# A routed LoRA, attention and nearest-neighbour chain on one core: distances in the two row halves of the array, keys early, dummy products first

## The chip, the core and the metric

The kernel runs on one core of a Trainium2 chip. The core has a matrix engine (TensorE, PE in the profile; its weight loads are shown apart as PEld), a vector engine (VectorE, DVE), a scalar engine (ScalarE, ACT), a general engine (GpSimd, POOL) and a queue that issues transfers (SyncE, SP). Each runs its own instructions in order and they meet at semaphores. The metric is the device time of one execution in microseconds (us), as the median of several.

## What is computed

There are 4 batches of 256 rows of 512 features (`x`), 64 context vectors of 512 features for each batch (`ctx`), four 256 x 256 matrices (`fside`) and a mask over the context vectors. In outline:

```
A   = ctx[0] + ctx[1] + ctx[2] + ctx[3]                             # 64 x 512
x   = x + 0.5 * sum_n softmax(x Rw^T + b)_n * ((x A^T) B_n^T)        # 8 experts, rank 64; then nan and inf are replaced
q, k, v = x Wq^T + bq,  ctx Wk^T + bk,  ctx Wv^T + bv               # 32 heads of 16
x   = layernorm(x + softmax(q k^T / 4, masked) v Wo^T + bo)
idx = for each of the 512 columns of ctx (64 numbers each): the 8 nearest columns
8 times, with matrix i mod 4:
    p = leaky_relu(x)                                              # x as 256 channels by 512 points
    x = x + (F_i p + F_i * (sum of p over the 8 neighbours)) / 9
```

The "points" of the last part are the 512 feature columns. Their positions are the columns of `ctx` of the same batch, 64 x 512. The neighbours are the same in all 8 rounds, so a 512 x 512 matrix of zeros, ones and (because each point is its own nearest neighbour and also enters on its own) twos on the diagonal, `nbr`, is made once for each batch, and each round is two matrix products.

## The kernel before

**The stages.** `mixture` and `mix` are the routed LoRA: `route` (x times router and summed A), on VectorE a softmax over experts and z (the softmax weights times the rank-64 part), z transposed (`zT`), `upd` with `lora_BT`, and x updated; hi, lo, odd and copy_predicated (L436 to L440) replace nan and inf, hi + lo on POOL. `x1T` is x transposed for the queries. `keys` makes `kT` and from it the block-wise keys `kbd` for all batches at once; `values`, `queries` and `attention` follow for each batch: scores `s` as row-quarter products (four products of 32 rows side by side in the array, each with `tile_position`), softmax on VectorE and ScalarE with the last multiplication on POOL (L716), transposes `pT`, `avT`, `o` with Wo, layer norm (its last two operations on POOL, L784 and L785). `block` is one of the 8 rounds of a batch: p on VectorE (L798), `wp` = p times F (fp32, L809), its two parts as float32r: `wph` rounded on ScalarE (L822) and the rest `wpl` on VectorE (L825), `blk` = both parts times `nbr` (L840), x updated (L852).

**The distances.** `nearest` (L459) makes `nbr`. The eight nearest columns m of a column n are those with the largest x_n . x_m - |x_m|^2 / 2. For this the moving operand `cxx` holds the 64 rows of ctx and below them their squares (ScalarE, L460), and the weights `cxl` hold the 64 rows again (a copy on POOL, L461) and below them -0.5 (set by POOL, L280). One fp32 product with 128 rows per 128 columns n, two passes in the profile, gives the tile `d` (L469). VectorE takes the eight largest of each row (`top`) and replaces them by a very low number (`rest`), ScalarE makes ones of these (`near`, bf16), TensorE transposes them and adds the diagonal (`nbrT`, L499 and L501), and ScalarE stores `nbr`. A batch has four tiles `d`.

**The order.** No order is written by hand. `Plan` (L57) records every operation with its engine, a cost, what it reads and what it writes. `emit` then goes through them as a list scheduler: for each engine it finds the operations that could start first (by the end of what they depend on, plus `SEEN[engine]`, a latency that is counted where a result is used on another engine), takes among these the one with the lowest rank, and of the engines' choices the earliest. The rank is `DEADLINES[batch]` less the longest remaining chain of work in that batch (for all operations of a round, of that round), so a batch with a low due time goes first. PSUM has 8 banks; an operation that needs one waits until one is free, and a second count, "stage", says how many may be held by tiles of everything but the block stage. Loads are all issued on SP in the order in which they are written (L253 to L274), and each waits for the one eight before it.

**The start.** The first load is 64 rows of ctx of batch 0. `d` of batch 0 needs it squared and copied. `route` of batch 0 needs its xT and the summed A. Each of the four pieces of Wk (`WkT`, 256 KB) holds 128 input features for all outputs, so that the first `kT` needs all four.

Of the kernel before, what the change touches and what calls it, by code (L numbers as in the profile page):

```python
# [8 lines left out]
F32 = mybir.dt.float32  # L9
BF16 = mybir.dt.bfloat16  # L10
F32R = mybir.dt.float32r
U8 = mybir.dt.uint8
I32 = mybir.dt.int32
AF = mybir.ActivationFunctionType
ALU = mybir.AluOpType
AX = mybir.AxisListType

B, S, H = 4, 256, 512
V, R = 64, 64
# [3 lines left out]
NC = H // 128  # L23
# [5 lines left out]
SLOPE = 0.01  # L29
LN_EPS = 1e-5  # L30
LOW = -3.0e38
DEADLINES = (0.0, 5.0, 10.0, 15.0)

SEEN = {"PE": 0.2, "ACT": 0.15, "DVE": 0.1, "POOL": 0.12, "SP": 0.0}


LANES = 8
RATE = 0.3  # L40

# [15 lines left out]
class Plan:  # L57
# [33 lines left out]
    def emit(self, deadline):  # L91
        longest = {}
        for op in reversed(self.ops):
            op.tail = op.cost + max(
                [o.tail + (SEEN[op.eng] if o.eng != op.eng else 0.0) for o in op.after if o.batch == op.batch],
                default=0.0,
# [6 lines left out]
        for op in self.ops:  # L103
            if op.rank is None:
                op.rank = deadline[op.batch] - longest.get(op.unit, op.tail)
        free = dict.fromkeys(SEEN, 0.0)
        ready = [op for op in self.ops if not op.todo]
# [47 lines left out]
def xattn_seq_kernel(ctx: ExitStack, tc: tile.TileContext, a: dict, out: bass.AP):  # L155
    nc = tc.nc
    V_, G_, A_, T_, S_ = nc.vector, nc.gpsimd, nc.scalar, nc.tensor, nc.sync

    const = ctx.enter_context(tc.tile_pool(name="const", bufs=1))
    keep = ctx.enter_context(tc.tile_pool(name="keep", bufs=1))  # L160
    work = ctx.enter_context(tc.tile_pool(name="work", bufs=1))
    small = ctx.enter_context(tc.tile_pool(name="small", bufs=1))
# [3 lines left out]
    shapes = {  # L166
        "bank": (psum, [128, 512], F32, 8),
        "xT": (keep, [128, NC, S], F32, 3),
        "s": (work, [128, H], F32, 8),
        "pT": (work, [128, H], F32, 4),  # L170
        "half": (work, [128, H], F32, 5),
        "full": (work, [128, 2, H], F32, 4),
        "wp": (work, [128, 2 * S], F32R, 8),
        "near": (work, [128, H], BF16, 5),
# [4 lines left out]
    def make(kind, place, name):  # L179
        pool, shape, dtype, _ = shapes[kind]  # L180
        return pool.tile(shape, dtype, tag=f"{kind}{place}", name=name)

    plan = Plan({kind: n for kind, (_, _, _, n) in shapes.items()} | {"stage": 8}, make)
    pe, act, dve, pool = (
        lambda *args, _e=e, **kw: plan.add(_e, *args, **kw) for e in ("PE", "ACT", "DVE", "POOL")
    )
# [4 lines left out]

    cxl = [keep.tile([128, H], F32, name=f"cxl{b}") for b in range(B)]
    cxx = [keep.tile([128, H], F32, name=f"cxx{b}") for b in range(B)]
    WkT = [keep.tile([128, H], F32, name=f"WkT{c}") for c in range(NC)]
    nbr = {}
    nbr_tag = [
        [f"nbr0_{k}" for k in range(4)],
        [f"WkT{k}" for k in range(4)],  # L200
        ["cxl0", "cxx0", "cxl1", "cxx1"],
        ["cxl2", "cxx2", "cxl3", "cxx3"],
    ]
    ctxT = keep.tile([128, NC, B, V], F32, name="ctxT")

# [18 lines left out]
    hsel2 = const.tile([128, 2], F32, name="hsel2")  # L224
    ones = const.tile([128, 128], BF16, name="ones")
    eps = const.tile([128, 1], F32, name="eps")
    above = const.tile([128, 1], F32, name="above")

    mbias = const.tile([128, B, V], BF16, name="mbias")
# [5 lines left out]
    def load(key, mb, dst, src, after=()):  # L235
        loads.append(key)
        plan.add("SP", 0.45, lambda: S_.dma_start(out=dst(), in_=src), after, (key,), rank=len(loads) - 1e4, load=mb)
# [9 lines left out]
    def load_x(b):  # L247
        load(("x", b), 0.5, lambda: x1[b].rearrange("p l h -> p (l h)"), a["x"][b])
# [1 line left out]
    def load_w(n):  # L250
        load(n, 1.0, lambda: w[n].rearrange("p c o -> p (c o)"), a[n])

    load(("cxx", 0), 0.13, lambda: cxx[0][0:64], a["ctx"][0])  # L253
    load("ctxT", 0.5, lambda: ctxT.rearrange("p c b v -> p (c b v)"), a["ctxT"])
    load("small", 0.05, lambda: consts, a["small"])
    load_xT(0)
    load(("cxx", 1), 0.13, lambda: cxx[1][0:64], a["ctx"][1])
    load_w("lora_BT")
    load_x(0)
    for b in range(2, B):  # L260
        load(("cxx", b), 0.13, lambda b=b: cxx[b][0:64], a["ctx"][b])
    for c in range(NC):
        load(("WkT", c), 0.25, lambda c=c: WkT[c], a["WkT"][:, bass.ts(c, H)])
    load_w("WqT")
    load("mask_i", 0.12, lambda: mask_i.rearrange("p b v -> p (b v)"), a["mask"].partition_broadcast(128))
    load_w("WvT")
# [7 lines left out]
    load_x(2)  # L274


    pool(0.5, lambda: make_identity(nc, ident), (), ("ident",))
    pool(0.3, lambda: G_.tensor_copy(ident_h, ident), ("ident",), ("ident_h",))
    for b in range(B):
        pool(0.5, lambda b=b: G_.memset(cxl[b][64:128], -0.5), (), (("cxl1", b),))  # L280
    pool(0.1, lambda: G_.memset(hsel, 1.0), (), ("hsel",))
    pool(
        0.4,
# [18 lines left out]
        ("hsel",),  # L302
        ("hsel2",),
    )
    pool(0.2, lambda: G_.memset(ones, 1.0), (), ("ones",))
    pool(0.1, lambda: G_.memset(eps, LN_EPS), (), ("eps",))
    pool(0.1, lambda: G_.memset(above, 1.0 + LOW * 2.0**-123), (), ("above",))  # L307
    for k in range(2):
# [148 lines left out]


    def nearest(b):  # L459
        act(0.6, lambda: A_.activation(cxx[b][64:128], cxx[b][0:64], AF.Square), (("cxx", b),), (("sq", b),))  # L460
        pool(0.6, lambda: G_.tensor_copy(cxl[b][0:64], cxx[b][0:64]), (("cxx", b),), (("cxl", b),))  # L461
        nears = []
        for j in range(H // 128):

            ps, top = Buf("bank", f"d2_{b}_{j}", "stage"), Buf("small", f"top{b}_{j}")
            rest, near = Buf("half", f"rest{b}_{j}"), Buf("near", f"near{b}_{j}")
            pe(
                0.87,
                lambda ps=ps, j=j: T_.matmul(  # L469
                    ps.tile, lhsT=cxl[b][:, bass.ts(j, 128)], rhs=cxx[b], start=True, stop=True  # L470
                ),
                (("sq", b), ("cxl", b), ("cxl1", b)),
                (ps, ("d2", b, j)),
            )
            dve(0.69, lambda ps=ps, top=top: V_.max(top.tile[:, 0:KNN], ps.tile), (ps,), (top,))
            dve(
                0.76,
                lambda ps=ps, top=top, rest=rest: V_.match_replace(rest.tile, top.tile[:, 0:KNN], ps.tile, LOW),
                (ps, top),
                (rest,),  # L480
            )

            act(
                0.62,
                lambda rest=rest, near=near: A_.activation(
                    near.tile, rest.tile, AF.Relu, bias=above, scale=-(2.0**-123)
                ),
                (rest, "above"),
                (near,),
            )  # L490
            nears.append(near)
        for k in range(H // 128):

            ps = Buf("bank", f"nbrT{b}_{k}", "stage")

            def turn(ps=ps, k=k):
                for j in range(H // 128):
                    o = ps.tile[:, bass.ts(j, 128)]
                    T_.matmul(o, lhsT=nears[j].tile[:, bass.ts(k, 128)], rhs=ident_h, start=True, stop=(j != k))  # L499
                    if j == k:  # L500
                        T_.matmul(o, lhsT=ident_h, rhs=ident_h, start=False, stop=True)  # L501

            def store(ps=ps, k=k):
                nbr[b, k] = keep.tile([128, H], F32R, tag=nbr_tag[b][k], name=f"nbr{b}_{k}")
                A_.copy(nbr[b, k], ps.tile)


            gone = [("kT", o) for o in range(NC)] if b == 1 else []
            if b > 1:
                gone = [("d2", i, j) for i in (2 * b - 4, 2 * b - 3) for j in range(H // 128)]  # L510
            pe(0.4, turn, (*nears, "ident_h"), (ps,))
            act(0.6, store, (ps, *gone), (("nbr", b, k),))


    def keys():
        for o in range(NC):
            ps, kT = Buf("bank", f"kT{o}", "stage"), Buf("half", f"kT{o}")
            pe(
                1.73,
                lambda ps=ps, o=o: [  # L520
                    T_.matmul(  # L521
                        ps.tile[:, 0 : B * V],
                        lhsT=WkT[c][:, bass.ts(o, 128)],
                        rhs=ctxT[:, c].rearrange("p b v -> p (b v)"),
                        start=(c == 0),
                        stop=(c == NC - 1),
                    )
                    for c in range(NC)
                ],
                (*(("WkT", c) for c in range(NC)), "ctxT"),  # L530
                (ps, ("kT", o)),
            )
            act(
                0.47,
                lambda ps=ps, kT=kT, o=o: A_.activation(
                    kT.tile[:, 0 : B * V], ps.tile[:, 0 : B * V], AF.Identity, bias=bqk[:, 1, o : o + 1]
                ),
                (ps, "small"),
                (kT,),
            )  # L540
            for k in range(2):
                pool(
                    0.95,
                    lambda kT=kT, o=o, k=k: G_.tensor_scalar(
                        kbd[:, o, :, k, :],
                        kT.tile[:, 0 : B * V].rearrange("p (b v) -> p b v", v=V),
                        hsel2[:, k : k + 1],
                        None,
                        ALU.mult,
                    ),  # L550
                    (kT, "hsel2"),
                    (("kbd", o, k),),
                )
# [315 lines left out]
    for b in range(B):  # L869
# [11 lines left out]
        plan.unit = None  # L881
    plan.emit(DEADLINES)

# [46 lines left out]
```

## Time and profile before

| what | us |
|---|---|
| median of 3 runs | 407.8 (407.43 to 408.28) |
| the profiled execution's own time | 408.37 |
| its span, first to last instruction | 406.7 |
| TensorE busy | 397.7 |
| VectorE busy | 275.9 |
| ScalarE busy | 122.2 |
| POOL busy | 93.8 |
| TensorE, `d` of all batches | 17.6 (32 passes, overlaps counted twice) |
| TensorE, `blk` (both parts) | 208.0 |
| TensorE, `wp` | 116.5 |

The profile is of one execution. A row of the page's fifth part gives a group of like instructions: their line, engine and operation, what they write and read, the shapes, how many there are, their busy time, the mean time of one, and the idle time of the engine ahead of them with what ended it. The chain of waits follows the work back from the last instruction, each time to what released it. A timeline row gives start and length of one instruction or of a run of like ones. Durations of products overlap in the pipeline, so the distance from start to start says what one costs.

### The profile page before, as it was taken

Reading aid. Unit: us, or ns where it says so; the run is one execution under the profiler, and the core shown is the slowest. Engines: PE = TensorE matmul, PEld = TensorE weight load, DVE = VectorE, ACT = ScalarE, POOL = GpSimd, SP = SyncE. Lnnn points to the kernel's source line nnn. Section 1 sums busy time; section 2 is a strip of 40 time slices with the busy share of each in tenths; the row PEclk is TensorE's granted clock in tenths of the full one; section 3 lists DMA queues with packets and bytes.
Section 4 is the critical chain, followed back from the end, with each engine's and each line's share of the span. In section 5 each row is a group of like instructions: output and inputs, shape, how many; then the busy total and the mean of one; then the engine's idle time right before and its main releaser. Section 6 shows DMA issues by size and latency. Waiting matters only on the chain.

```text
span 406.7 us, 5695 instructions
## 1 busy us (share of the span) xinstructions
PE 397.7 (98%) x2288; PEld 305.2 (75%) x2288; DVE 275.9 (68%) x474; ACT 122.2 (30%) x225; POOL 93.8 (23%) x98
## 2 busy tenths in 40 slices
PE   5999999999999999999999999999999999999996
PEld 2677676868676657776877888888888888888884
DVE  2947859989978998948667556555465655636452
ACT  3604226344646463512304211211111121111211
POOL 7139113295727319801300000000000000000000
PEclk9999999999999999999999999999999999999999
DMA  7995100000000000000000000000000000010102
GB/s 247 336 413 208 53 0 2 0 2 2 2 0 2 2 2 1 2 1 2 0 0 2 0 0 2 0 2 0 0 2 0 0 2 0 0 53 0 52 6 99
DMA packets 4666, 15.20 MB, mean 37 GB/s; under 512 B 672, under 2 KB 800, under 8 KB 4000
## 3 DMA queue, kind: packets, MB, share of 16 engines
q1 hardware_dynamic: 4640, 14.84, 10.2%
q8 instruction: 18, 0.29, 0.3%
q14 instruction: 8, 0.07, 0.1%
HBM read 12.74 MB, written 2.10 MB: 36 GB/s over the span
## 4 chain that ended last, share of the span: by engine, by line
PE 95%; ACT 2%; DVE 2%; DMA 1%; issue 0%; POOL 0%; DVEq 0%; ACTq 0%
PE blk L840 29%; PE wp L809 27%; PE q L613 7%; PE upd L415 7%; PE o L760 6%; PE d L469 4%; PE pT L728 3%; PE v L575 2%; PE route L359 2%; PE kT L521 2%; PE s L654 2%; PE avT L740 1%; PE zT L405 1%; PE x1T L444 1%; DVE p L798 1%; PE nbrT L499 1%
## 5 line engine op out<-in xcount | busy, mean ns | idle before, releaser
L809 PE MATMUL wp<-fT,p 128*128 128x256 f32 x512 | 116.5, 380 | 0.2 <-DVE p L798 0.2
L809 PEld LDWEIGHTS wp<-fT,p 128*128 128x128 f32 x512 | 96.7, 190 | 16.3 <-issue 1.8
L840 PE MATMUL blk<-nbr,wph 128*128 128x512 f32 x256 | 107.3, 419 | 0.0
L840 PE MATMUL blk<-nbr,wpl 128*128 128x512 f32 x256 | 100.7, 393 | 0.0
L822 ACT CAST wph<-wp 128x512 fp32r<-128x512 f32 x64 | 37.5, 586 | 167.7 <-PE wp L809 167.7
L825 DVE TENSOR_TENSOR wpl<-wp,wph 128x512 fp32r<-128x512 f32 x64 | 44.2, 690 | 49.1 <-ACT wph L822 49.0
L852 DVE SCALAR_TENSOR_TENSOR x<-blk,x 128x512 f32<-128x512 f32 x64 | 44.0, 687 | 47.6 <-PE blk L840 47.5
L840 PEld LDWEIGHTS blk<-nbr,wph 128*128 128x128 f32 x256 | 48.2, 188 | 10.9 <-issue 0.2
L840 PEld LDWEIGHTS blk<-nbr,wpl 128*128 128x128 f32 x256 | 48.2, 188 | 10.8 <-DVE wpl L825 0.5
L798 DVE SCALAR_TENSOR_TENSOR p<-x 128x512 f32<-128x512 f32 x64 | 48.4, 761 | 2.2 <-POOL x L785 0.4
L716 POOL TENSOR_TENSOR s<-s,rden 128x512 f32<-128x512 f32 x32 | 34.9, 1123 | 36.8 <-DVE rden L707 36.8
L760 PE MATMUL o<-WoT,avTs 128*128 128x512 f32 x64 | 29.8, 596 | 0.3 <-ACT avTs L754 0.3
L613 PE MATMUL q<-x1T,WqT 128*128 128x256 f32 x128 | 29.1, 383 | 0.3 <-DVE s L686 0.3
L415 PE MATMUL upd<-lora_BT,zTs 128*128 128x512 f32 x64 | 28.9, 599 | 0.0
L613 PEld LDWEIGHTS q<-x1T,WqT 128*128 128x128 f32 x128 | 23.9, 190 | 4.4 <-DVE s L686 0.5
L680 DVE TENSOR_REDUCE mx<-s 128x8 f32<-128x512 f32 x32 | 19.8, 677 | 4.5 <-PE s L654 4.5
L415 PEld LDWEIGHTS upd<-lora_BT,zTs 128*128 128x128 f32 x64 | 11.8, 190 | 13.5 <-issue 12.4
L469 PE MATMUL d<-cxx,cxl 128*128 128x512 f32 x32 | 17.6, 692 | 4.3 <-POOL above L307 4.3
L695 DVE TENSOR_REDUCE den<-s 128x8 f32<-128x512 f32 x32 | 20.1, 673 | 1.3 <-ACT s L692 1.3
L686 DVE TENSOR_TENSOR s<-s,mx 128x512 f32<-128x512 f32 x32 | 19.9, 677 | 0.4 <-issue 0.3
L733 ACT COPY pTs<-pT 128x512 f32<-128x512 f32 x32 | 16.8, 600 | 11.0 <-PE pT L728 11.0
L692 ACT ACTIVATE s<-s 128x512 f32<-128x512 f32 x32 | 18.4, 640 | 4.8 <-DVE s L686 4.8
(89 smaller groups left out, 361.5 us busy)
## 6 DMA issues: line engine op xcount, KB each, us to landing
xT<-in_xT SPq DMA_DIRECT2D x4, 512.0 KB, 8.2
x<-in_x SPq DMA_DIRECT2D x4, 512.0 KB, 12.0
out<-x SPq DMA_DIRECT2D x8, 256.0 KB, 2.0
lora_BT<-in_lora_BT SPq DMA_DIRECT2D x1, 1024.0 KB, 7.7
WkT<-in_WkT SPq DMA_DIRECT2D x4, 256.0 KB, 9.3
WqT<-in_WqT SPq DMA_DIRECT2D x1, 1024.0 KB, 9.0
WvT<-in_WvT SPq DMA_DIRECT2D x1, 1024.0 KB, 9.3
rows<-in_rows SPq DMA_DIRECT2D x2, 512.0 KB, 11.9
```

The costliest lines, as they stand in the source:

```text
L415: T_.matmul(ps2.tile, lhsT=zT.tile[:, bass.ts(c, 128)], rhs=w["lora_BT"][:, c, :], start=(c == 0), stop=(c == NC - 1),)
L469: lambda ps=ps, j=j: T_.matmul(ps.tile, lhsT=cxl[b][:, bass.ts(j, 128)], rhs=cxx[b], start=True, stop=True),
L613: T_.matmul(ps.tile[:, 0:S], lhsT=w["WqT"][:, c, bass.ts(o, 128)], rhs=x1T[b].tile[:, c, :], start=(c == 0), stop=(c == NC - 1),)
L695: lambda s=s, g=g: V_.tensor_reduce(den.tile[:, bass.ts(g, HPC)], heads(s), AX.X, ALU.add),
L716: lambda s=s, g=g: G_.tensor_tensor(heads(s), heads(s), rden.tile[:, bass.ts(g, HPC)].unsqueeze(2).to_broadcast([128, HPC, V]), ALU.mult,),
L760: T_.matmul(po.tile, lhsT=avT.tile[:, bass.ts(c, 128)], rhs=w["WoT"][:, c, :], start=(c == 0), stop=(c == NC - 1),)
L798: lambda l=l: V_.scalar_tensor_tensor(p.tile[:, l], pt[:, l], SLOPE, pt[:, l], ALU.mult, ALU.max),
L809: T_.matmul(ps.tile[:, bass.ts(k, S)], lhsT=p.tile[:, c, bass.ts(2 * m2 + k, 128)], rhs=wi[:, c, :], start=(c == 0), stop=(c == NL - 1),)
L822: act(0.59, lambda ps=ps, hi=hi: A_.copy(hi.tile, ps.tile), (ps,), (hi,))
L825: lambda ps=ps, hi=hi, lo=lo: V_.tensor_tensor(lo.tile, ps.tile, hi.tile.bitcast(F32), ALU.subtract),
L840: T_.matmul(pb[o].tile, lhsT=part.tile[:, bass.ds(m % 2 * S + o * 128, 128)], rhs=nbr[b, m], start=(m == 0 and k == 0), stop=(m == H // 12 ...
L852: lambda o=o: V_.scalar_tensor_tensor(pt[:, o], pb[o].tile, 1.0 / (KNN + 1.0), pt[:, o], ALU.mult, ALU.add),
```

## The change

The distances: the product is taken apart. The cross term x_n . x_m has only 64 rows, so two tiles `d` are made side by side, one in rows 0 to 63 of the array and one in rows 64 to 127; `cxx` therefore holds the same 64 rows twice (for batch 0 by a load that reads them twice, for the others by a copy on ScalarE). The squares go into `sq`, and are split into a rounded float32r part (ScalarE) and the rest (VectorE for batch 0, POOL for the others), 64 rows each, in `csq`. A product of a constant -0.5 (`mhalf_r`, 128 x 128) with `csq` adds them to each `d` in float32r. The cross products are two operations of the plan, each for two tiles, and the four products with `mhalf_r` one each.

The keys: `WkT` is laid out by outputs, so that piece o holds all inputs for the outputs of `kT` o; each `kT` waits for its own piece alone. The first two pieces are loaded right behind xT of batch 0, the others behind x of batch 0.

The first work: `ones` is the first constant in the text, and TensorE gets 20 products of `ones` with itself (128 x 128, bf16) into a bank that nothing reads.

The plan: other `DEADLINES`, greater `SEEN`, 7 instead of 8 banks for "stage". The memory that `nbr` of batches 1 to 3 takes over is named accordingly (`csq` in place of `cxl`).

```diff
-DEADLINES = (0.0, 5.0, 10.0, 15.0)
+DEADLINES = (0.0, 30.0, 50.0, 57.0)
-SEEN = {"PE": 0.2, "ACT": 0.15, "DVE": 0.1, "POOL": 0.12, "SP": 0.0}
+SEEN = {"PE": 0.25, "ACT": 0.3, "DVE": 0.25, "POOL": 0.3, "SP": 0.0}
+WARM = 20
...
-    plan = Plan({kind: n for kind, (_, _, _, n) in shapes.items()} | {"stage": 8}, make)
+    plan = Plan({kind: n for kind, (_, _, _, n) in shapes.items()} | {"stage": 7}, make)
...
-    cxl = [keep.tile([128, H], F32, name=f"cxl{b}") for b in range(B)]
+    csq = [keep.tile([128, H], F32R, name=f"csq{b}") for b in range(B)]
...
-    load(("cxx", 0), 0.13, lambda: cxx[0][0:64], a["ctx"][0])
+    def load_k(o):
+        load(("WkT", o), 0.25, lambda: WkT[o], a["WkT"][:, bass.ts(o, H)])
+
+    def load_points(b):
+        load(("cxx", b), 0.13, lambda: cxx[b][0:64], a["ctx"][b])
+
+    load(("cxx", 0), 0.26, lambda: cxx[0], a["ctx"][0].unsqueeze(0).to_broadcast([2, V, H]))
     load("ctxT", 0.5, lambda: ctxT.rearrange("p c b v -> p (c b v)"), a["ctxT"])
     load("small", 0.05, lambda: consts, a["small"])
     load_xT(0)
-    load(("cxx", 1), 0.13, lambda: cxx[1][0:64], a["ctx"][1])
+    load_k(0)
+    load_points(1)
+    load_k(1)
     load_w("lora_BT")
     load_x(0)
+    load_k(2)
+    load_k(3)
     for b in range(2, B):
-        load(("cxx", b), 0.13, lambda b=b: cxx[b][0:64], a["ctx"][b])
-    for c in range(NC):
-        load(("WkT", c), 0.25, lambda c=c: WkT[c], a["WkT"][:, bass.ts(c, H)])
+        load_points(b)
     load_w("WqT")
...
+    pool(0.2, lambda: G_.memset(ones, 1.0), (), ("ones",))
+
+    idle = Buf("bank", "idle")
+    pe(
+        2.2,
+        lambda: [
+            T_.matmul(idle.tile[:, 0:128], lhsT=ones, rhs=ones, start=True, stop=True) for _ in range(WARM)
+        ],
+        ("ones",),
+        (idle,),
+    )
...
-    for b in range(B):
-        pool(0.5, lambda b=b: G_.memset(cxl[b][64:128], -0.5), (), (("cxl1", b),))
+    pool(0.2, lambda: G_.memset(mhalf, -0.5), (), ("mhalf",))
+    pool(0.3, lambda: G_.tensor_copy(mhalf_r, mhalf), ("mhalf",), ("mhalf_r",))
...
     def nearest(b):
-        act(0.6, lambda: A_.activation(cxx[b][64:128], cxx[b][0:64], AF.Square), (("cxx", b),), (("sq", b),))
-        pool(0.6, lambda: G_.tensor_copy(cxl[b][0:64], cxx[b][0:64]), (("cxx", b),), (("cxl", b),))
-        nears = []
+        sq = Buf("half", f"sq{b}")
+        if b:
+            act(0.6, lambda: A_.copy(cxx[b][64:128], cxx[b][0:64]), (("cxx", b),), (("cxx2", b),))
+        act(0.6, lambda: A_.activation(sq.tile[0:64], cxx[b][0:64], AF.Square), (("cxx", b),), (sq,))
+        act(0.6, lambda: A_.copy(csq[b][0:64], sq.tile[0:64]), (sq,), (("csq", b),))
+        (pool if b else dve)(
+            1.15 if b else 0.69,
+            lambda: (G_ if b else V_).tensor_tensor(csq[b][64:128], sq.tile[0:64], csq[b][0:64].bitcast(F32), ALU.subtract),
+            (sq, ("csq", b)),
+            (("csq2", b),),
+        )
+        nears, dist = [], [Buf("bank", f"d2_{b}_{j}", "stage") for j in range(H // 128)]
+        for k in range(2):
+            def cross(k=k):
+                for j in (2 * k, 2 * k + 1):
+                    r = slice(64 * (j % 2), 64 * (j % 2) + 64)
+                    T_.matmul(
+                        dist[j].tile,
+                        lhsT=cxx[b][r, bass.ts(j, 128)],
+                        rhs=cxx[b][r],
+                        start=True,
+                        stop=False,
+                        tile_position=(64 * (j % 2), 0),
+                    )
+            pe(0.9, cross, (("cxx", b), ("cxx2", b)), (dist[2 * k], dist[2 * k + 1], ("d2", b, k)))
+            for j in (2 * k, 2 * k + 1):
+                pe(
+                    0.24,
+                    lambda j=j: T_.matmul(dist[j].tile, lhsT=mhalf_r, rhs=csq[b], start=False, stop=True),
+                    (("csq", b), ("csq2", b), "mhalf_r"),
+                    (dist[j], ("d2", b, 2 + j)),
+                )
         for j in range(H // 128):
-            ps, top = Buf("bank", f"d2_{b}_{j}", "stage"), Buf("small", f"top{b}_{j}")
+            ps, top = dist[j], Buf("small", f"top{b}_{j}")
-            pe(
-                0.87,
-                lambda ps=ps, j=j: T_.matmul(
-                    ps.tile, lhsT=cxl[b][:, bass.ts(j, 128)], rhs=cxx[b], start=True, stop=True
-                ),
-                (("sq", b), ("cxl", b), ("cxl1", b)),
-                (ps, ("d2", b, j)),
-            )
...
                     T_.matmul(
                         ps.tile[:, 0 : B * V],
-                        lhsT=WkT[c][:, bass.ts(o, 128)],
+                        lhsT=WkT[o][:, bass.ts(c, 128)],
...
-                (*(("WkT", c) for c in range(NC)), "ctxT"),
+                (("WkT", o), "ctxT"),
...
+    laid["WkT"] = g["L1_xattn_Wk"].reshape(NC, 128, NC, 128).transpose(3, 0, 2, 1).reshape(128, -1)
```

## The prediction

> **What bounds the kernel now.** I read the page's first part first: it shows which engine has no slack.
>
> ```profile
> PE 397.7 (98%) x2288; PEld 305.2 (75%) x2288; DVE 275.9 (68%) x474; ACT 122.2 (30%) x225; POOL 93.8 (23%) x98
> ```
>
> TensorE is busy 397.7 of 406.7 us. Next the waits, for what is left of it.
>
> ```profile
> PE d L469 <- POOL above L307: 4.3, 1, 4.3
> PE o L760 <- ACT avTs L754: 0.3, 1, 0.3
> PE q L613 <- DVE s L686: 0.3, 1, 0.3
> PE wp L809 <- DVE p L798: 0.2, 1, 0.2
> ```
>
> Its one long wait is the start, 4.3 us; the others, with the weight loads that they hold up, cost about 1.3 us. The end is the third loss: after the last product one VectorE operation and the store of the output.
>
> ```profile
> 4.30 6.39 PE d L469 x8
> 10.69 1.74 PE route L359 x16
> 12.43 3.48 PE d L469 x8
> ...
> 16.47 0.88 PE zT L405 x8
> ...
> 39.68 1.72 PE upd L415 x4
> ...
> 63.45 0.89 PE s L654 x32
> 64.34 1.91 PE upd L415 x4
> ...
> 155.60 3.67 PE blk L840 x16
> ```
>
> These rows of the chain of waits give start, length and count of each piece. The same eight passes of `d` take 6.39 us at 4.30 and 3.48 us at 12.43: TensorE runs at half speed at first. Weight loads of `d` show when it changes:
>
> ```profile
> 8.69 0.34 PEld L469 LDWEIGHTS d<-cxx,cxl 128*128 128x128 f32 x1 [0.52 <-issue]
> 9.55 0.31 PEld L469 LDWEIGHTS d<-cxx,cxl 128*128 128x128 f32 x1 [0.52 <-issue]
> 10.10 0.19 PEld L359 LDWEIGHTS route<-rw,xT 128*128 128x128 f32 x1 [0.24 <-issue]
> ```
>
> They are .86 apart, then .55; later .43. So full speed came near 9.8, about 5.5 us after the first product. Last, a table by stage: columns are busy time of PE, PEld, DVE, ACT, POOL.
>
> ```profile
> 40.00:80.00 40.00, 39.95 (x281) 28.97 (x280) 32.34 (x68) 16.10 (x32) 8.49 (x7) 1.00 0.05 14
> 80.00:130.00 50.00, 49.72 (x474) 35.63 (x473) 45.22 (x78) 27.27 (x52) 35.05 (x30) 1.00 0.01 2
> 215.00:403.00 188.00, 187.88 (x854) 158.15 (x852) 103.53 (x158) 35.00 (x60) 0.00 (x0) 1.00 0.03 9
> ```
>
> VectorE is 90% busy from 80 to 130 and 55% in the block stage. It is the engine that can come to hold TensorE up. A row of its own timeline shows how, where POOL runs too:
>
> ```profile
> 86.91 0.41 DVE L436 TENSOR_SCALAR hi<-x 128x512 f32<-128x512 f32 x1
> 87.24 1.27 DVE L437 TENSOR_SCALAR lo<-x 128x512 f32<-128x512 f32 x1
> ```
>
> Two operations of one size: .41 alone, 1.27 while POOL's `s` runs. The block's `p` likewise takes .69 in most of its 64 runs, up to 1.78 beside POOL.
>
> So the time is: start 4.3 us, TensorE's work, some stalls, and the tail. The sum below is of changes to these against the profiled execution, 408.37 us (1.7 more than its span); the median of the runs shown is 407.8, and I subtract from that.
>
> **The start.** Before, `d` of batch 0 waits for its load (landed 3.54) and POOL's copy (3.60 to 4.20). After, the copy is gone: the load itself fills both halves, 256 KB instead of 128. Loads of 256 KB land .67 us apart further on (Wk), so 3.54 becomes 3.7 to 4.1. The 20 dummies need `ones` alone, set by POOL at about 2.1 by the order of its constants. A bf16 product 128 wide takes .056 at full speed (the `nbrT` pieces: five in .28), so .11 at half: 2.2 us, until 4.3. The first `d` therefore starts about when it did. What is gained is clock: 5.5 us from 2.1 gives full speed at 7.6 instead of 9.8.
>
> Here a rule bears on it. The Trainium skill, "TensorE: Matmul & The Clock Gate", Part 1, gives a free-running window of about 3.4 us, so the change comes one to two windows after the first product: 5.5 to 8.9 for us; the row before (5.5 us after) lies within that. By the row d's products are done at 8.7 (below); by the late end at 9.2; by the early end at 7 or so, where they would wait for the next load anyhow. I take the row; the late end costs .5.
>
> Batch 0's `d`: eight half-array passes in pairs, four pass times. At half speed .86 each, from 4.35: 3.3 us to 7.7. Then four f32r products at the block's price (16 in 3.67 to 3.72 us: .23 each), .93: to 8.7. Their operand: Square .63, ACT's copy .6, VectorE's subtraction .69 from 3.9 on: 5.9, hidden by 1.8. VectorE is idle there.
>
> `route` needs xT0, landed at 8.15 before. 128 KB more ahead of it cost .3 (Wk's rate) to .8 (the rate from ctxT 4.90 to xT0): 8.5 to 8.9. So route runs from 8.8 to 10.55. Now kT0 and kT1 fill TensorE (eight passes of 256 columns each, .216: 3.45 us) to 14.0; their weights and cxx1 are the next 640 KB behind xT0, 1.7 us at Wk's rate, so in by 10.3, while kT1 starts at 12.3. Before, all four Wk pieces had to land (17.7), hence keys at 24.8. Then the first pair of `d` of batch 1 (.86) and its mode change: 15.1. Transposing z has to wait for VectorE: before, z ended 3.2 us after route's end; with a second 0.67-us replacement put before it, and POOL beside it, 4 to 5 us, so zT starts near 15.6 instead of 16.47: **−.87**. lora_BT is moved behind 512 KB of Wk: 11.13 becomes about 14.4, still ahead of its use at 17.
>
> **The work after zT.** kT0 and kT1 are done: −3.45. Half of nbrT of batch 0, done by then before, is not: +.5. Of batch 1, a pair (.86) and four f32r (.93) remain: +1.79. Batches 2 and 3: 8×.43 = 3.44 become 2×.86 + 4×.23 = 2.65 each: −1.58. That halves run at once I take from the scores: 32 row-quarter products in .89, where one alone (like a transpose, .11) would make 3.5.
>
> A rule speaks against it: the Trainium skill, "TensorEngine Tiling (Array Packing)", Key Properties: changing the tiling mode drains the engine. Row: after the scores four passes of `upd` take 1.91, 1.72 otherwise (.19); entering adds about .1. So .3 a visit. Six visits (batches 1 and 2 have their pairs apart), one inside the start and one ahead of zT; four here: +1.2. Were the drain free this would be 0; at .4 it is 1.6. Sum: **−1.54**.
>
> The other edits have cover. Batches 1 to 3 get ACT's extra copy and copy-rounding (.6 each; ACT is 30% busy) and a POOL subtraction (about 1.27, as L438) instead of a copy (.60). Four POOL memsets of .52 go. One of eight banks is closed to all but block and dummies; the neighbours' tiles move to other memory, last read long before.
>
> **The stalls.** With the new due times and latencies the emitted order puts batch 0's blocks early: its first `wp` comes near 94 us (151.7 before), between the attention of the later batches. Following that order with the durations above, I find two stalls. At about 80 us x1T of batch 1 is late (1.7): VectorE has been without a pause since the scores at 49, and POOL's four `s` (1.04 each) stand ahead of hi (1.27), for which VectorE's copy_predicated waits; behind it x1T, q and everything of that attention. At about 130 us blk of batch 0 waits .8 for wpl, queued on VectorE behind two p, two x, two hi, two lo and two odd, while POOL holds it up. Others make .3. That is 2.8, but the same walk makes the worst of before 1.4, where the trace has .3 to .4 at 88 us: I take 2.0, 1.3 at best, 2.8 and more at worst. Against 1.3: **+.7**. Price of an early p that meets POOL: 1.0 on VectorE, on TensorE only where its slack is gone.
>
> The tail is the same wp, blk, x of batch 3 and store: 0. Sum −.87 −1.54 +.7 = −1.7: the profiled execution 406.7, the median **406.1**.
>
> **Rivals.**
> (a) Stalls no more than before, drains cheaper: −2.4 −.4: 405.0. For it: in the mixed stage VectorE's share should fall between 90% and 55%. Against: the POOL rows.
> (b) No measurable change. A measurement of this kernel tells about 0.2% (.8 us). Needs .9 us back: visits at .4 (.6 with the two early ones) and xT0 later by .5, or the walk's 2.8. Then about 407.3.
> (c) The end on the other side: VectorE with POOL becomes the bound where batch 0's blocks meet attention. TensorE then stalls at each block: 20 p before POOL falls idle, each up to 1.0 longer, and TensorE gets a third of it, 6 us of stalls. That makes −2.4 −1.3 +6 = +2.3: 410.1. It decides from stalls of 4.5 us on (−2.4 −1.3 +4.5 = +.8). Against: a block gives VectorE 6×.69 = 4.1 us of work for 7.2 of TensorE's.
> (d) The halves don't run at once: eight more pass times of .86: +6.9, 413.0. The scores' row speaks against it.
>
> **How the numbers follow.** Forecast 406.1: .40, own range 405.2 to 407.1. (a) .13, (b) .22, (c) .19, (d) .06. Below 407.0: (a) and nearly all of the forecast, .52; within .2%: .23; slower: (c), (d), .25. The range goes from (a) less .5 to (c)'s middle: 404.5 to 410.0.
>
> **What would show it.** Right: the first `d` near 4.3 but its loads at full pace from about 7.6; kT before zT, zT at 15 to 16; pairs of L501 at .86 for two; first wp at 90 to 97; TensorE's stalls after 20 us near 2 us in all, at x1T and blk; other lengths unchanged. Wrong: pairs taking 1.7; first `d` later than 4.6; wp or x1T waiting for VectorE many times between 80 and 215; a tail longer than 3.8 us.

## The result

The changed kernel takes 419.58 us (median of 5 runs, 419.50 to 420.14) against 407.8 for the kernel before: a ratio of 1.0293, with a 95% interval of 1.0278 to 1.0308. It is slower by 11.8 us where 1.7 less was forecast. Its profiled execution has a span of 418.4 us. First its page, as for the kernel before:

```profile
PE 401.6 (96%) x2324; PEld 307.5 (73%) x2324; DVE 280.3 (67%) x475; ACT 131.2 (31%) x234; POOL 99.4 (24%) x95
```

TensorE has 3.9 us more of busy time in a span 11.7 longer: most of the loss is idle time. The waits say where:

```profile
PE d L501 <- DMA cxx<-in_ctx: 6.2, 1, 6.2
PE blk L886 <- DVE wpl L871: 2.1, 1, 2.1
PE x1T L466 <- DVE x L462: 2.1, 1, 2.1
```

One wait of 6.2 us for the first load, and two of 2.1 for VectorE. The chain of waits shows the first:

```profile
0.78 9.77 DMA cxx<-in_ctx
10.60 3.78 PE d L501 x8
14.38 1.78 PE d L514 x4
16.16 1.74 PE route L381 x16
17.89 3.50 PE kT L567 x16
21.40 1.06 PE d L501 x4
22.46 1.02 PE zT L427 x8
```

The first load lands 9.77 us after its issue (2.75 before), so `d` starts at 10.6 instead of 4.3, and `zT` at 22.46 instead of 16.47: 6.0 us of the loss are there by then. From here on the new work is cheaper than the old, and yet 5.7 more are lost. The table by stage (after the stretch and its length the busy time of PE, PEld, DVE, ACT and POOL, then the granted clock):

```profile
60.00:100.00 40.00, 37.45 (x259) 23.08 (x258) 39.25 (x68) 18.32 (x34) 20.34 (x17) 1.00 0.00 1
142.10:145.40 3.30, 3.30 (x10) 2.52 (x9) 0.69 (x1) 0.00 (x0) 0.32 (x1) 0.50 0.00 0
```

The kernel before had in the first of these stretches:

```profile
60.00:100.00 40.00, 39.67 (x318) 29.25 (x317) 37.37 (x70) 18.11 (x37) 20.81 (x18) 1.00 0.00 1
```

From 60 to 100 VectorE is now busy for 39.25 of 40 us and TensorE for 37.45: VectorE has no slack left there and TensorE waits, which points to VectorE as the one that sets the pace. The second row has a granted clock of .50: after the wait for wpl, which ended at 140.69, TensorE ran at half speed for 3.4 us, with no idle time shown. By estimate that costs another 1.7, half of the stretch. VectorE's own timeline ahead of that wait, and the row of POOL that lies beside it:

```profile
133.06 1.06 DVE L458 TENSOR_SCALAR hi<-x 128x512 f32<-128x512 f32 x1
134.05 1.26 DVE L459 TENSOR_SCALAR lo<-x 128x512 f32<-128x512 f32 x1
135.23 1.26 DVE L458 TENSOR_SCALAR hi<-x 128x512 f32<-128x512 f32 x1
136.41 1.26 DVE L459 TENSOR_SCALAR lo<-x 128x512 f32<-128x512 f32 x1
137.59 2.44 DVE L461 TENSOR_SCALAR odd<-x 128x512 uint8<-128x512 f32 x2
139.96 1.28 DVE L871 TENSOR_TENSOR wpl<-wp,wph 128x512 fp32r<-128x512 f32 x2
...
129.82 9.93 POOL L762 TENSOR_TENSOR s<-s,rden 128x512 f32<-128x512 f32 x8 [2.66 <-DVE rden L753]
```

Six operations that take .42 each when alone take 1.1 to 1.3 each, one after the other, while POOL works through its `s`; wpl stands behind them.

### The profile page after: what moved, and what is told of

It reads as the page before. It is cut to its first block, busy times and chain, and to the rows that moved or that the text cites. A ratio compares the mean times of both kernels' runs of the same rounds, so it can differ in the third digit from the quotient of the medians.

```text
span 418.4 us, 5743 instructions
## 1 busy us (share of the span) xinstructions
PE 401.6 (96%) x2324; PEld 307.5 (73%) x2324; DVE 280.3 (67%) x475; ACT 131.2 (31%) x234; POOL 99.4 (24%) x95
## 4 chain that ended last, share of the span: by engine, by line
PE 86%; DVE 10%; DMA 2%; ACT 0%; issue 0%; ACTq 0%
PE blk L886 29%; PE wp L855 26%; PE o L806 6%; PE q L659 5%; PE upd L437 4%; PE pT L774 2%; DMA cxx<-in_ctx 2%; PE d L501 2%; PE v L621 2%; PE kT L567 2%; PE route L381 2%; PE s L700 1%; PE avT L786 1%; DVE den L741 1%; DVE lo L459 1%; DVE odd L461 1%
## 5 line engine op out<-in xcount | busy, mean ns | idle before, releaser
L855 PE MATMUL wp<-fT,p 128*128 128x256 f32 x512 | 119.2, 380 | 0.0
L886 PE MATMUL blk<-nbr,wph 128*128 128x512 f32 x256 | 111.4, 435 | 0.0
L898 DVE SCALAR_TENSOR_TENSOR x<-blk,x 128x512 f32<-128x512 f32 x64 | 43.0, 686 | 23.7 <-PE blk L886 23.7
L844 DVE SCALAR_TENSOR_TENSOR p<-x 128x512 f32<-128x512 f32 x64 | 51.5, 831 | 4.6 <-POOL x L831 4.0
L762 POOL TENSOR_TENSOR s<-s,rden 128x512 f32<-128x512 f32 x32 | 38.5, 1235 | 67.1 <-DVE rden L753 44.2
L830 POOL TENSOR_TENSOR x<-x,rows 128x512 f32<-128x512 f32 x8 | 10.7, 1336 | 48.3 <-DVE x L826 45.5
L806 PEld LDWEIGHTS o<-WoT,avTs 128*128 128x128 f32 x64 | 11.7, 190 | 12.0 <-issue 11.8
## 6 DMA issues: line engine op xcount, KB each, us to landing
xT<-in_xT SPq DMA_DIRECT2D x4, 512.0 KB, 10.6
WkT<-in_WkT SPq DMA_DIRECT2D x4, 256.0 KB, 10.6
```

The costliest lines, as they stand in the source:

```text
L762: lambda s=s, g=g: G_.tensor_tensor(heads(s), heads(s), rden.tile[:, bass.ts(g, HPC)].unsqueeze(2).to_broadcast([128, HPC, V]), ALU.mult,),
L806: T_.matmul(po.tile, lhsT=avT.tile[:, bass.ts(c, 128)], rhs=w["WoT"][:, c, :], start=(c == 0), stop=(c == NC - 1),)
L844: lambda l=l: V_.scalar_tensor_tensor(p.tile[:, l], pt[:, l], SLOPE, pt[:, l], ALU.mult, ALU.max),
L855: T_.matmul(ps.tile[:, bass.ts(k, S)], lhsT=p.tile[:, c, bass.ts(2 * m2 + k, 128)], rhs=wi[:, c, :], start=(c == 0), stop=(c == NL - 1),)
L886: T_.matmul(pb[o].tile, lhsT=part.tile[:, bass.ds(m % 2 * S + o * 128, 128)], rhs=nbr[b, m], start=(m == 0 and k == 0), stop=(m == H // 12 ...
L898: lambda o=o: V_.scalar_tensor_tensor(pt[:, o], pb[o].tile, 1.0 / (KNN + 1.0), pt[:, o], ALU.mult, ALU.add),
```

## Experiments

Two causes were open after the traces, the first load and VectorE, and a third that would have explained the loss without either: that the new order by itself, with the early blocks, is all of it.

**The first load as two.** It was issued as two loads of 64 rows in place of one that reads 64 rows twice; the engines' orders are otherwise those of the changed kernel.

```diff
-    load(("cxx", 0), 0.26, lambda: cxx[0], a["ctx"][0].unsqueeze(0).to_broadcast([2, V, H]))
+    ... plan.add("SP", 0.45, lambda: [S_.dma_start(out=cxx[0][64 * k : 64 * k + 64], in_=a["ctx"][0]) for k in range(2)], ...)
```

> The changed kernel with its first load issued as two loads of 64 rows, one to each half of cxx, in place of one load that reads the 64 rows twice; every engine's order is otherwise that of the changed kernel. Theory A (the one load is carried by two of the sixteen transfer engines, holds them for some 8 us and makes every load behind it late): the first d starts near 4.4 us instead of 10.6, route near 9 instead of 16.2, and the time falls by 5.5 to 7 to about 413; what stays above 407.8 is VectorE's and POOL's doing between 60 and 145 us. Rival B (twice the bytes are simply slow, or the dummies hold TensorE): first d still at 9 to 10.6, time 418 to 420. Rival C (a late start is made up later because the middle is bound by VectorE): first d early, time still above 417.

Measured: 414.19 us, 1.0144 (1.0114 to 1.0174).

```profile
4.36 3.79 PE L501 MATMUL d<-cxx 64*128 64x512 f32 x8
```

5.4 us are gone, hardly less than theory A's 5.5 to 7; B and C fall. The two waits of 2.1 for VectorE and one stretch at half clock are still there.

**The same in the kernel before.** Only the first load was replaced.

```diff
-    load(("cxx", 0), 0.13, lambda: cxx[0][0:64], a["ctx"][0])
+    load(("cxx", 0), 0.26, lambda: cxx[0], a["ctx"][0].unsqueeze(0).to_broadcast([2, V, H]))
```

> The kernel before with its first load alone replaced by the one that reads the 64 rows twice (the second half is overwritten by the squares as always). Theory A: first d near 10.7 instead of 4.3, time 407.8 + 5.5 to 6.5, about 413 to 414.5. Rival B in the form that 128 KB more cost their transfer time: +.3 to .8, about 408.4. Rival C (made up later): 408 to 410.

Measured: 415.14 us, 1.0176 (1.0157 to 1.0195): 7.0 more. The start of its chain of waits:

```profile
0.79 10.34 DMA cxx<-in_ctx
...
11.88 5.67 PE d L469 x8
17.54 1.74 PE route L359 x16
```

Against 4.30 and 10.69 before, route starts 6.85 later, and nothing of it is made good later: the span is 6.8 longer.

**One plain load of 256 KB.** The 64 rows were laid twice in memory, so that one load of 128 rows brings the same bytes.

```diff
+    ... "ctx0_twice": np.concatenate([ctx[0], ctx[0]]),
-    load(("cxx", 0), 0.26, lambda: cxx[0], a["ctx"][0].unsqueeze(0).to_broadcast([2, V, H]))
+    load(("cxx", 0), 0.26, lambda: cxx[0], a["ctx0_twice"])
```

> The changed kernel with the 64 rows laid twice in memory, so that the first load is one plain load of 128 rows and 256 KB; orders unchanged. Theory A (what is slow is the doubled reading, whose pattern has two as its outermost count, so that two of the sixteen engines carry it): like two loads, first d near 4.4, about 413 to 414.5. Rival B (one load of 256 KB ahead of all others is slow): first d at 9 to 10.6, 418 to 420.

Measured: 413.51 us, 1.0141 (1.0115 to 1.0168).

```profile
4.43 3.71 PE d L501 x8
8.15 1.18 PE d L514 x4
9.33 1.74 PE route L381 x16
...
15.63 1.02 PE zT L427 x8
```

So it is neither the bytes nor their being one load, and two loads that read the rows twice were fast as well: what is slow is the doubled reading in one pattern. The traces' records of landing signals fit this. The plain load of 256 KB has sixteen of them, at 2.85 to 3.60 us; the doubled one of the changed kernel has three, at 1.85, 10.29 and 10.55. For ctxT, the load behind it, fourteen came at 4.9 to 5.3 us and two at 11.9. The records name no engines, but this is what would be seen if two of sixteen transfer engines carried the whole first load, and every load behind it were complete only when those two were free. The Trainium skill, "DMA: Bandwidth & Descriptors", Rules for kernel authors, says the first of these of a pattern whose outermost dimension is small, and names the leading broadcast of c copies: it is confined to at most c engines. This case's number is 9.8 us from issue to landing, instead of 2.8 for the plain 256 KB.

**The old due times and latencies in the changed kernel**, with its own first load, and with two loads.

```diff
-DEADLINES = (0.0, 30.0, 50.0, 57.0)
+DEADLINES = (0.0, 5.0, 10.0, 15.0)
-SEEN = {"PE": 0.25, "ACT": 0.3, "DVE": 0.25, "POOL": 0.3, "SP": 0.0}
+SEEN = {"PE": 0.2, "ACT": 0.15, "DVE": 0.1, "POOL": 0.12, "SP": 0.0}
```

> The changed kernel with the due times and latencies of the kernel before, its slow first load kept. Theory A with the second half (the new order puts batch 0's blocks into the stage in which VectorE has no slack, which costs 2.1 at x1T, 2.4 at blk and 1.7 of half clock after it, less 1.3 of stalls before): the start stays late, first d at 10.6, the middle has stalls of 1 to 2 us, time about 413 to 414.5. Rival C: 417 or more. Rival D (the new order alone is the loss): about 408.

> Both edits at once: two loads, and the due times and latencies of before. If the two causes are independent and all: 419.6 less 6 less 5.5 to 6.5, so 406.5 to 408. If the new distances cost more on TensorE than they save (drains dearer than .3): 409 to 411. If the order was needed for the early keys: 410 or more.

Measured: 421.18 us (1.0326, 1.0309 to 1.0343) and 416.51 (1.0221, 1.0194 to 1.0248). The expectation that the new order costs 5 to 7 us here fails in both: the old due times are no better than the new but worse, by 1.3 to 1.6 us with the slow first load and by 2.3 with two loads. The times lie in the rivals' open ranges ("417 or more", "410 or more"), but do not show the rivals' reasons. The first wp is back at 148 to 153 us, and TensorE still waits for VectorE, at other places (x1T three times, blk, s, and with two loads zT). VectorE is therefore late without the early blocks too.

**The new due times, latencies and seven banks in the kernel before.**

> The kernel before with the changed kernel's due times, latencies and seven banks alone. Theory D (the new order by itself brings batch 0's blocks into the stage in which VectorE has no slack): stalls of TensorE at x1T or blk between 60 and 145 us, 411 to 414. Rival E (VectorE's queue only comes under strain because keys and scores come earlier in the changed kernel): 407 to 409.

Measured: 422.04 us, 1.0337 (1.0323 to 1.0351), the dearest of the single parts. One wait makes most of it:

```profile
PE pT L728 <- DVE z L387: 8.4, 1, 8.4
```

The transposes at the head of TensorE's queue were released last by z, which had den, hi, lo, odd and copy_predicated of other work ahead of it on VectorE. The granted clock is half from 70.6 to 77.4; the last 3.3 us of this lie behind the wait. Theory D has the sign, at more than twice the size, and not at x1T or blk.

**The distances alone, and the keys alone, in the kernel before.** The first takes over `nearest` with two first loads, the second the layout of Wk and the order of the first loads.

> The kernel before with the changed distances alone (row halves, float32r squares, the first load as two); due times, latencies, keys and loads else as before. Theory I (the distances are worth what the rows show, two to three us of TensorE's time less .3 for each change of mode): 406 to 407.5. Theory H (the planner answers other costs with another order of everything behind them, and VectorE's lack of slack makes most orders dear): a stall of several us somewhere between 15 and 110 us, 411 to 418.

> The kernel before with the keys' part alone: Wk by outputs, its loads and the order of the first loads as in the changed kernel (the first load still 64 rows). Theory I: nothing is waited for there, 407.5 to 408.3. Theory H: 409 to 412.

Measured: 419.24 us (1.0292, 1.0228 to 1.0356) and 411.98 (1.0103, 1.0084 to 1.0122). Theory H in both, the first beyond its range. The first one's four runs fall in two pairs: 417.4 and 417.7 at a mean granted clock of .996, 420.8 and 423.3 at .988. In its trace the longest wait is again for VectorE:

```profile
PE zT L405 <- DVE s L710: 5.3, 1, 5.3
```

VectorE worked off a long run of `mx` and then of `s` ahead of it. Each of three parts that should be neutral or good costs 4 to 14 us when added alone to the kernel before, where the planner answers each with another order. For the plan and the distances the trace shows a long wait for VectorE. For the keys it shows none above .8 us, and how their 3.9 us come about was not followed.

**The dummies alone in the kernel before**, every order kept.

> The kernel before with the 20 dummy products alone, every engine's order otherwise unchanged. If the clock follows from the first product and d of batch 0 is not held up: full speed at 7.6 to 8.4 instead of 9.8, d of batch 0 done at 9.4 to 9.8 instead of 10.7, and the time less by .9 to 1.3 (about 406.8). Rival: the dummies end after 4.3 or the gain is lost again where z of batch 0 is waited for: 407.8, no difference.

Measured: 408.03 us, .9994 (.9987 to 1.0001), 21 runs: no difference. PE's timeline of this run:

```profile
2.13 2.32 PE L305 MATMUL idle<-ones 128*128 128x128 bf16 x20 [2.13 <-POOL ones L305]
4.24 4.11 PE L469 MATMUL d<-cxx,cxl 128*128 128x512 f32 x8
8.18 1.90 PE L359 MATMUL route<-rw,xT 128*128 128x72 f32 x16
...
16.49 0.33 PE L499 MATMUL nbrT<-ident_h,near 128*128 128x128 bf16 x3 [1.49 <-ACT nbr L505]
...
16.98 1.56 PE L415 MATMUL upd<-lora_BT,zTs 128*128 128x512 f32 x3
```

The clock came at 5.1, and route starts 2.35 earlier than before. Just ahead of 16.49 TensorE then waits 1.49 for ScalarE, which in order has the squares of batch 3 ahead, whose load lands at 15.2. `upd` starts at 16.98 instead of 17.64. That is the rival's mechanism, at another place: most of the gain is lost at a wait for something else. The .7 that are left at `upd` do not show in the median, whose interval ends at .5 less; where they go was not followed.

**VectorE: less work in the same order.** The replacement of nan and inf (four operations on VectorE: hi, lo, odd, copy_predicated; one on POOL, the addition) was left out of the two-load version and of the kernel before.

```diff
-        dve(0.42, lambda: V_.tensor_scalar(hi.tile, v, 0.0, 1e4, ALU.max, ALU.min), (key,), (hi,))
+        dve(0.42, lambda: None, (key,), (hi,))
 ... lo, odd, copy_predicated and POOL's hi likewise
```

> The two-load version without the replacement of nan and inf (five operations for each of the eight row tiles: four on VectorE, one on POOL), every order otherwise unchanged; it leaves out that part of the computation. Theory F (what is left above the time before is TensorE waiting for VectorE and POOL, at x1T behind hi, lo, odd and at blk behind wpl): these stalls and the half-clock stretch after them go, 5 to 8 less than the two-load version, 406 to 409. Rival G (it is TensorE's own work: drains, narrow products): less than 1.5 of it goes, 412.5 or more.

> The kernel before without the replacement of nan and inf, order otherwise unchanged; it leaves out that part of the computation. Its stalls for VectorE are 1.3 in all, so theory F gives 406.5 to 407.8. If VectorE held it up in ways that the waits do not show, it would be 405 or less.

Measured: 406.10 us (.9947, .9932 to .9963) and 407.22 (.9982, .9975 to .9989). The two-load version gains 8.1, the kernel before .9. In the first no wait of TensorE for VectorE but .3 is left, and no stretch at half clock:

```profile
PE idle L295 <- POOL ones L289: 2.1, 1, 2.1
PE zT L427 <- DVE z L409: 0.3, 1, 0.3
```

Theory F stands. Like for like, the changed kernel in this pair is 1.1 us faster than the old (1.4 by the ratios, give or take .7): this is what the change was worth, in its new order, with the load mended and VectorE out of the way.

**POOL's turns.** POOL's 32 multiplications of `s` were left out of the two-load version.

> The two-load version without POOL's 32 multiplications of s by the reciprocal sums, every other instruction and order unchanged; it leaves out the division of the softmax. VectorE's own work is the same. Theory L (VectorE is late because its SBUF operations take turns with POOL's s, hi, lo, odd at 1.2 us each instead of .42): the stalls at x1T and blk and the half-clock stretch go, 405.5 to 408. Rival M (VectorE simply has too much to do there, POOL or not): the stalls stay, 411 or more.

Measured: 406.88 us, .9978 (.9966 to .9989): 7.3 less, with VectorE's work as it was. The groups of hi, lo and odd, first in the kernel before, then in the changed one, then in this run:

```profile
L437 DVE TENSOR_SCALAR lo<-x 128x512 f32<-128x512 f32 x8 | 5.3, 661 | 0.0
...
L436 DVE TENSOR_SCALAR hi<-x 128x512 f32<-128x512 f32 x8 | 4.8, 597 | 0.3
...
L439 DVE TENSOR_SCALAR odd<-x 128x512 uint8<-128x512 f32 x8 | 3.1, 403 | 0.0
```

```profile
L459 DVE TENSOR_SCALAR lo<-x 128x512 f32<-128x512 f32 x8 | 6.9, 869 | 0.0
L461 DVE TENSOR_SCALAR odd<-x 128x512 uint8<-128x512 f32 x8 | 6.6, 838 | 0.0
...
L458 DVE TENSOR_SCALAR hi<-x 128x512 f32<-128x512 f32 x8 | 6.6, 827 | 0.2
```

```profile
L461 DVE TENSOR_SCALAR odd<-x 128x512 uint8<-128x512 f32 x8 | 4.3, 554 | 0.0
...
L458 DVE TENSOR_SCALAR hi<-x 128x512 f32<-128x512 f32 x8 | 3.6, 455 | 0.2
...
L459 DVE TENSOR_SCALAR lo<-x 128x512 f32<-128x512 f32 x8 | 3.4, 419 | 0.0
```

The last figure ahead of the second bar is the mean of one in ns. `odd` keeps its length of .4 in the kernel before (403), so it never met POOL's work there, and it does in the changed one (838). VectorE's busy time falls from 280.6 us in the two-load version to 267.6 in this run, with the same operations. This run also shortens the way from softmax to transposes, so it does not say how much of the 7.3 is due to the turns alone.

**Taking the turns away without the work** was tried by giving hi, lo and odd an interleaved order of elements.

```diff
-V_.tensor_scalar(hi.tile, v, 0.0, 1e4, ALU.max, ALU.min)
+V_.tensor_scalar(hi.tile.rearrange("p (a b) -> p b a", a=2), v.rearrange("p (a b) -> p b a", a=2), 0.0, 1e4, ALU.max, ALU.min)
```

> The two-load version in which hi, lo and odd read and write their rows in another order (two interleaved halves, 1 KB apart, instead of one run); same values, same work, every order unchanged. Theory L (these three are the ones that take turns with POOL, and only in their contiguous form): each takes about .69 whether POOL works or not, instead of .42 or 1.2, POOL's s goes back to 1.05; the stalls at x1T and blk shrink to 1 or less, 405.5 to 407.5. Theory N (removing s helped only because pT no longer waited for POOL, or the load on VectorE counts): the operations get longer by .27 and the time stays at 413 or rises.

> The kernel before with hi, lo and odd in the same interleaved form, order unchanged. Theory L: it has few of these meetings (means of .60, .66, .40 against .42 alone), so .27 more on each and fewer turns nearly cancel: 406.8 to 408.2. Theory N: 408.2 or more.

Measured: 424.15 us (1.0405, 1.0371 to 1.0439) and 411.40 (1.0085, 1.0070 to 1.0101). The assumption behind theory L's form was wrong: interleaved, hi and lo take .65 and odd 1.3 when alone, and all still take turns with POOL (1.5 and 2.15). What the pair shows is a dose. By their means the three operations take 10.9 us more in all in the two-load version and 12.2 in the kernel before; the first pays 10.0 for it, the second 3.2. About 3.4 of the 10.0 is clock, by estimate: this run's trace has 10.2 us at half clock in mid-kernel, that of the two-load version 3.4. POOL's operations beside them grow longer too (`hi` from 1.36 to 1.80, `s` from 1.23 to 1.32 in the mean), so the dose is one for both engines. In the changed order nearly all of it comes out as time; in the order before, about a quarter does.

```profile
PE x1T L466 <- DVE x L462: 4.5, 3, 2.9
PE blk L886 <- DVE wpl L871: 4.3, 1, 4.3
```

These are the two waits of the changed kernel, doubled, in the two-load interleaved run (x1T now three times, 2.9 at the longest). None of the runs that compute everything is clearly faster than the kernel before.

## Why the prediction was wrong

The median can be followed along the runs: 419.6, less 5.4 (the first load mended) is 414.2; less 8.1 (VectorE relieved) is 406.1; plus 1.1 (the old work and order in its place) is 407.2; plus .9 (VectorE's share there) is 408.1, the kernel before as measured beside them. So +11.8 is +5.4 for the load, +7.2 for VectorE (8.1 less .9) and −1.1 for the rest; the .3 that are missing are the kernel before, 407.8 beside the changed one and 408.1 beside the others.

- "so 3.54 becomes 3.7 to 4.1": **the first step that failed.** It took the landing of a load of 256 KB from Wk, a plain load of 128 rows. The first load's pattern is another one, and it landed at 10.55. The edit was costed by its bytes alone; the page cited above, which has the rule, was not weighed.
- "gives full speed at 7.6": in the changed kernel 15.8: after the dummies TensorE was idle until 10.6, and `d` ran at half speed (3.78 for four pass times). With the load mended 8.4 and 8.2, in the old order with two loads 7.6, with the dummies alone 5.1. So from 3.0 to 6.3 us after the first product where I took 5.5; the range estimated from the clock page's window, 5.5 to 8.9, holds 8.4, 8.2 and 7.6 but not 5.1.
- "zT starts near 15.6": 22.5 in the changed kernel, by the first step. With two loads 16.1, with one plain load 15.6: right, for the mended kernel.
- Halves at once, and .3 a visit: right. A pair takes 1.06 (.86 and .2), and eight passes of batch 3 take 1.92. Rival (d) is out. Here the tiling page's drain was worth weighing: the .2 of a visit, and the 1.02 of `zT` between two pairs against .88 before, come to the .3 that was counted.
- "−.87 −1.54", so −2.4: the like-for-like pair gives −1.1. The mechanism was right; a term was missing and one too large. In that pair `zT` starts .4 earlier (16.31 against 16.70) instead of .87. And blocks of several batches now alternate more: 55 groups of blk instead of 33, and in the trace the first float32r product after fp32 ones takes .42 to the next instead of .23. From start to start, blk takes 3.2 us more in the relieved two-load version than in the relieved kernel before and wp 1.9 less, 231.8 together instead of 230.6: +1.2.
- "I take 2.0" for stalls: **the second step that failed.** Both places were right, x1T at 80 and blk at 130, down to the queue in front of wpl. The size was not. The walk took its durations from the order before, where `odd` takes .40, none of its eight runs having met POOL, and it counted POOL's `s` at 1.04. Where both engines have a queue they alternate instead, 1.2 us for each pair (`s` 1.235 in the mean). Then I scaled the walk's 2.8 down because it had overstated one stall of the kernel before. And no step had the clock: beside one of the two waits of 2.1 stood 3.4 us of half speed, 1.7 more. It is +7.2 instead of +.7.
- Rival (c) named the right mechanism and side, VectorE with POOL, and gave 410.1; it erred in the place (two waits and a stretch at half clock, not each block) and in laying it on the early blocks: the old due times leave the blocks late and lose more. Its sum, too, had nothing for the first load.
- The tail was as before, wp, blk, x, as forecast.

How much of the 7.2 is POOL's turns and how much VectorE's work as such stays open. That VectorE together with POOL is the bound there is shown, by removing work of both, by removing work of POOL's alone and by adding to both.

## What to carry to other kernels

Cost a load by its pattern before its bytes: here a pattern with an outermost count of two landed after 9.8 us instead of 2.8, and every load queued behind it was complete only later still. Where an order comes from a list scheduler and a second engine is about 90% busy over a long stretch, as VectorE is here, expect no edit to be local: walk the new order with the durations that operations have beside their neighbours, not their means in the old order, and count a wait of 2 us on TensorE with the half-clock stretch that may follow. A pair of runs that relieves the suspected engine in both kernels tells in one step what an edit's own work is worth and what its order costs.

## What the hardware showed unasked

Stretches of half clock in mid-kernel last 3.41 us or twice that (6.83 in two runs), and come with waits of TensorE of about 2 us or more. In the two-load version the wait of 2.1 that ended at 82.3 was followed by half clock from 83.5, and that of 2.1 for wpl, which ended at 136.1, by none. In the changed kernel it is the other way round: none behind the wait that ended at 88.6, half clock from 142.05 behind the one that ended at 140.7. So beyond its own length the same wait can cost 1.7 us or nothing. The fastest of the four two-load runs, 412.22 us, has a mean granted clock of .998, the others (413.96 to 414.79) .995. The Trainium skill, "TensorE: Matmul & The Clock Gate", Part 1, has the length (a free-running window of about 3.4 us), and puts the danger at one idle window; here shorter gaps were enough. And the interleaved order of elements: a tensor_scalar of 128 x 512 in fp32 takes .65 us instead of .42, with one byte out 1.3.
